# Block 1's v, q and g by three passes of split operands, in place of plain float32 matmuls

## The chip, the core and the metric

The kernel runs on one core of a Trainium2 chip. The metric is the device time of one execution in microseconds; before the change it is 929.19 us, the median of three runs (929.16 to 929.43).

## The reference

The input x is 4 sequences of 1024 tokens with 512 features, float32. Two sublayers follow each other, each with a layer norm before and after it and a residual sum:

```
h   = layernorm(x)
q, v, g = h @ Wq.T, h @ Wv.T, silu(h @ Wg.T)          # 512 x 512 each
ret = scan over tokens: state = lam * state + v       # lam per head of 32 features
out = (layernorm(q * ret) * gamma + beta) * g
x1  = x + layernorm(out @ Wo.T)

h2  = layernorm(x1)
f   = silu(h2 @ fp8(gate_w) * gate_s) * (h2 @ fp8(up_w) * up_s)   # 512 -> 1536
x2  = x1 + layernorm((f @ fp8(down_w)) * down_s)                  # 1536 -> 512
```

The FFN weights are rounded to an 8-bit float type and used as float32.

## The kernel before

The 4096 tokens are worked off in 8 blocks of 512 (TB). Each block goes through the first sublayer (class Retention) and then the FFN (class Ffn). The FFN of a block is a loop over 12 chunks of 128 hidden features (`for i in range(NI)`), in each of which TensorE does a gate group (pfg), an up group (pfu) and, two chunks later, a down group (pd), of 8 matmuls each. The work of the next block's first sublayer is placed by hand between the groups of this loop: `f` is the FFN of block t, `b` is the Retention of block t+1, `n` that of block t+2, and `l` is the FFN of the block before. All of it is in one program whose order is written out by hand: every engine takes its instructions in the order of the source (InOrder), so one instruction that waits holds up all that stand behind it on its engine, and SP issues all but a few DMAs in that order as well.

There are two ways to compute a product here. The plain one (project) multiplies float32 operands; blocks 0 and 1 use it for v, q, g and o (methods v, q, gate, o). The other one is by exact passes (begin, end, pass_of); blocks 2 to 7 use it. Each operand is cut into a top part (its upper mantissa bits), a low part (the rest) and a diff part (a combination of the two), of type F32R. `begin` does the top pass and the low pass into one bank of PSUM, after which ACT scales the bank by 1 + 4096; `end` adds the diff pass. A pass is four matmuls of 128x512. After `end`, v is scanned on DVE in two halves of 256, q is multiplied into y, and g goes through silu into the tile mids.

For the passes the weights must be split. Splitter does it in 16 units: n = 0 to 3 are the four 128-column chunks of v, 4 to 7 of q, 8 to 11 of g, 12 to 15 of o. `copy` copies a unit from its input to a DRAM tile (the top part), `split` computes low and diff by three DVE operations and one of ACT, `store` writes both to DRAM, and `keep` loads o's top and low. In the kernel before, the split overwrites the weights in SBUF (low takes the place of w), so a unit of v, q or g can be split only when block 1 has used it for the last time. The four units of o are split before the first FFN, and v, q, g during the FFN of block 0; two units of g are left for the FFN of block 1. From block 2 on, all parts are fetched from DRAM through a ring of four units (w_ring).

The FFN weights come in 18 pieces of 128x1024 (gate, up, down in turn; three pieces serve two chunks i). A piece is loaded into a scratch place (`parts[places[n]]`, seven places, of which four become the tile for x1nT of block 0 later), cast to the 8-bit type on DVE, and written as F32R into gate_sb, up_sb or down_sb by ACT. `rounds(k)` advances this by k steps, three to a piece. A piece whose place is taken is loaded when the piece before it in that place has been cast (load_next).

PSUM has eight banks: pa0 and pa1, two of pf, and pd0 to pd3. Gate and up of the FFN share the two pf banks: a gate group can start when ACT's silu has read the gate before it (or DVE the up before it), and so on in turn.

The order before the FFN of block 0 is: block 0's v and q; its g, interleaved with the transposition of block 1's x (turn_x, keep_x); block 1's v; block 0's o, one 128-token row set s after the other, with the moments of o (o_moments), the residual (x1_of), the moments of x1 (x1_moments), its normalised form (x1n_of) and its transposition (turn_x1n, upper_of, rest_of); and between these the first chunks of block 1's q. Pool does the variance roots and the residual sums. In the FFN of block 0 come the rest of block 1's q (i = 0, 1), the mean and g (i = 3 to 6), the normalisation of y (mean, center_y, var, rstd_y, z), and o (i = 7 to 10).

Of the kernel before, what the change touches and what calls it, by code (L numbers as in the profile page):

```python
# [23 lines left out]
def sandwich(  # L24
# [135 lines left out]
    places = [0, 4, 1, 5, 2, 6, 3] + [4 + n % 3 for n in range(len(pieces) - 7)]  # L160
# [169 lines left out]
    class Splitter:  # L330


        def __init__(self):
            self.sources = {"v": wvT, "q": wqT, "g": wgT, "o": woT}
            self.at_work = {}
# [7 lines left out]

        def copy(self, n):
            k, c = units[n]
            parts = operands[k, c] = {
                part: dram.tile([P, D], F32, tag=f"{part}_{k}{c}", name=f"d{part}_{k}{c}", bufs=1)
                for part in ("top", "low", "diff")
            }
            if k == "o":  # L350
                sp.dma_start(parts["top"], woT[ts(c, P), :])
            else:
                src = self.sources[k].rearrange("(c p) f -> p c f", p=P)[:, :, ts(c, P)]
                sp.dma_start(self.by_chunk(parts["top"]), src)

        def split(self, n):
            k, c = units[n]
            if k == "o":
                w, top, low = wo_sb[:, c], self.room[0], self.room[1]
            else:  # L360
                w = {"v": wv_sb, "q": wq_sb, "g": wg_sb}[k][:, :, ts(c, P)]
                top, low = self.by_chunk(self.room[n % 2]), w
            dve.tensor_scalar(top.bitcast(I32), w.bitcast(I32), TOP_MASK, None, ALU.bitwise_and)
            dve.tensor_tensor(low, w, top, ALU.subtract)
            dve.scalar_tensor_tensor(top, top, -LOW, low, ALU.mult, ALU.add)
            act.activation(low, low, AF.Copy, scale=1.0 / LOW)
            self.at_work[n] = top, low

        def store(self, n):
            k, c = units[n]  # L370
            for part, ap in zip(("diff", "low"), self.at_work.pop(n)):
                t = operands[k, c][part]
                sp.dma_start(t if k == "o" else self.by_chunk(t), ap)

        def keep(self, n):
            k, c = units[n]
            if c == 0:
                room = big.tile([P, 2, NC, D], F32R, tag="x1n0", name="wo_parts")
                wo_parts["top"], wo_parts["low"] = room[:, 0], room[:, 1]
            for part in ("top", "low"):  # L380
                sp.dma_start(wo_parts[part].bitcast(F32)[:, c], operands[k, c][part])

        times = {
            (0, 0, "start"): "k15 c0", (0, 0, "mid"): "s0", (0, 1, "start"): "k0", (0, 1, "mid"): "s1",
            (0, 1, "end"): "c1 c2", (0, 2, "start"): "k1 s2", (0, 2, "end"): "k2 c3",
            (0, 3, "end"): "s3 c4", (0, 4, "start"): "c5", (0, 4, "mid"): "k3 s4",
            (0, 4, "end"): "c6", (0, 5, "start"): "k4 s5", (0, 5, "mid"): "c7 k5", (0, 5, "end"): "s6 c8",
            (0, 6, "start"): "k6", (0, 6, "mid"): "s7 c9", (0, 6, "end"): "k7 s8",
            (0, 7, "start"): "s9", (0, 7, "mid"): "k8 k9", (0, 8, "end"): "c10", (0, 11, "end"): "c11",
            (1, 0, "start"): "r s10", (1, 0, "mid"): "s11 k10", (1, 0, "end"): "k11",  # L390
            (1, 2, "end"): "w12", (1, 3, "mid"): "w13", (1, 4, "mid"): "w14", (1, 5, "start"): "w15",
# [46 lines left out]
    class Retention:  # L438
# [7 lines left out]
        def __init__(self, t, xt=None):  # L446
# [6 lines left out]
            self.fast = t >= FAST  # L453
            self.bank, self.top, self.flipped = {}, {}, {}
# [16 lines left out]
        def new_xnT(self):  # L471
            kind = F32R if self.fast else F32
            self.xnT = big.tile([P, TB // Q, NC, Q], kind, tag="xnT", name=f"xnT_{self.t}")
# [25 lines left out]
        def keep_x(self, s, copy=act.copy):  # L499
            copy(self.by_chunk[:, :, ts(s, NQ)], self.ptx.pop(s).rearrange("p c (b j) -> p c b j", j=Q))  # L500

# [65 lines left out]
        def pass_of(self, bank, k, c, part):  # L567
            w = next_unit(k, c, part).rearrange("p (c f) -> p c f", c=NC)
# [8 lines left out]
            fetch_weights()  # L577
# [110 lines left out]
        def scan(self, c):  # L688
            home = big if self.t == 1 and c > 1 else work
            tag, bufs = ("fuse", 3) if home is big else ("ret", 2)  # L690
            self.ret[c] = ret = home.tile([P, TB], F32, tag=tag, name=f"ret_{self.t}_{c}", bufs=bufs)
# [83 lines left out]
        def silu(self, c):  # L775
            home = big if self.t == 0 and c == 3 else work
            tag, bufs = ("fuse", 3) if home is big else ("tok", 4) if self.t == 1 and c == 0 else ("sg", 3)
# [13 lines left out]
        def gate_y(self, c):  # L791
            y = self.y[:, c, :]
            if self.fast:
# [187 lines left out]
    for n in range(4):  # L981
        load_piece(n)
    wg_sb = load_square(wgT, "wg_sb")
# [5 lines left out]
    splitter = Splitter()  # L989
    splitter.new_room()  # L990
    a = Retention(0, x_first)
# [20 lines left out]
    b = Retention(1)  # L1012
    wo_sb = load_square(woT, "wo_sb")
    for n in range(4, 7):
        load_piece(n)
    a.v(0, "pf", later)
    a.scan(0)
    rounds(2)
# [4 lines left out]
    rounds(2)  # L1023
    a.q(1)
    a.y_of(1)
    rounds(2)
    a.v(2, "pf")
    a.scan(2)
    rounds(2)
    a.q(2)  # L1030
    a.y_of(2)
    rounds(2)
    a.v(3, "pf")
    a.scan(3)
    rounds(1)
    b.stats(0)
    a.q(3)
    a.y_of(3)
    for s in range(1, NS):
        b.stats(s)  # L1040
    splitter.copy(12)
    splitter.split(12)
    b.rstd()
    b.shift()
    a.g_of(0, "pf")
    a.mean()
    a.center_y()
    a.g_of(1, "pf")
    for s in range(NS):
        b.norm_x(s, True)  # L1050
    a.gate(2, "pf")
    b.new_xnT()
    for s in range(NS):
        b.turn_x(s, f"pd{s}")
    b.keep_x(0)
    b.keep_x(1)
    b.keep_x(2, dve.tensor_copy)
    b.keep_x(3, dve.tensor_copy)
    a.var()
    rounds(6)  # L1060
    a.rstd_y()
# [3 lines left out]
    splitter.store(12)  # L1065
    splitter.copy(13)
    b.v(0, "pf", early)
    b.v(0, "pf", later)
    for c in range(NC):
        a.z(c)  # L1070
    splitter.split(13)
    b.v(1, "pf")
    b.scan(0)
    b.v(2)
    b.scan(1)
    rounds(3)
    b.v(3, "pf")
    b.scan(2)
    rounds(1)
    b.scan(3)  # L1080
    splitter.store(13)
    splitter.copy(14)
    splitter.split(14)
    a.o(0, "pd0")
    a.o_moments(0)
    rounds(1)
    a.x1_of(0)
    a.o(1, "pd1")
    a.o_moments(1)
# [3 lines left out]
    a.o(2, "pd2")  # L1093
    a.o_moments(2)
    a.x1_moments(1)
    a.x1_of(2)
    a.x1n_of(1)
    a.o(3, "pd3")
    a.new_x1nT()
    a.turn_x1n(0)  # L1100
# [6 lines left out]
    b.q(0, "pf")  # L1107
    a.turn_x1n(1)
    a.upper_of(1)
    splitter.store(14)  # L1110
    splitter.copy(15)
    b.q(1, "pf", early)
    a.turn_x1n(2)
    a.upper_of(2)
    b.q(1, "pf", later)
    a.x1_moments(3)
    a.x1n_of(3)
    a.rest_of(1)
    b.y_of(0)
    a.rest_of(2)  # L1120
    rounds(2)
    a.turn_x1n(3)
    a.upper_of(3)
    b.q(2, "pd0", early)
    a.rest_of(3)
    rounds(1)
    b.y_of(1)
    splitter.split(15)

    l = None  # L1130
    for t in range(NB):
        f, n = Ffn(a), None
        fast = b is not None and b.fast
        for i in range(NI):
            if t > 0 and (t > 1 or i) and not (fast and i == 11):
                (f if i else l).rest((i - 1) % NI)
            if t == 0 and i == 0:
                n = Retention(2)
                rounds(3)
# [24 lines left out]
            if b and not fast and i == 5:  # L1164
                b.z(0)
            if b and not fast and i >= 8:
                b.x1_moments(i - 8)
            f.gate(i)
            if t == 0 and i in (5, 6):
                n.norm_x(2 * i - 10, True)  # L1170
                n.norm_x(2 * i - 9, True)
# [4 lines left out]
            if n and t == 0 and i == 7:  # L1176
# [20 lines left out]
            if b and t == 0 and i < 2:  # L1197
                b.q(i + 2, tokens=slice(None) if i else later)
                b.y_of(i + 2)
            if b and not fast and i == 3:  # L1200
                b.g_of(0)
                b.mean()
                b.center_y()
                n.stats(2)
# [3 lines left out]
            if b and not fast and i == 4:  # L1208
                rounds(3)
                b.g_of(1)  # L1210
                b.var()
            if b and not fast and i == 5:
                b.g_of(2)
                b.z(1)
            if b and not fast and i == 6:
                b.g_of(3)
                b.z(2)
                b.z(3)
            if b and not fast and 7 <= i <= 10:
                b.o(i - 7)  # L1220
            if b and not fast and i == 8:
                b.new_x1nT()
            if b and not fast and 8 <= i < 11:
                b.x1n_of(i - 8)
            if b and not fast and 8 <= i < 10:
                b.move_x1n(i - 8)()
            if b and not fast and 9 <= i < 11:
                b.upper_of(i - 9)
            if b and not fast and 7 <= i < 10:
                b.o_moments(i - 7)  # L1230
# [17 lines left out]
            if t == 0 and i == 10:  # L1248
# [3 lines left out]
            if b and i == 11:  # L1252
# [3 lines left out]
            if t == 0 and i == 11:  # L1256
# [8 lines left out]
            if t == 0 and i == 4:  # L1265
# [43 lines left out]
            if n and t == 0 and i in (8, 9):  # L1309
                n.low_of(2 * i - 16)  # L1310
                n.low_of(2 * i - 15)
            if n and t == 0 and i == 10:
# [9 lines left out]
            if t == 0:  # L1322
                if i == 3:
                    rounds(2)
                    b.halves()
                    rounds(1)
                elif i < 8:
                    rounds(3)
                if i == 2:
                    b.halves()  # L1330
# [10 lines left out]
            if n and i == 6:  # L1341
                n.new_xnT()
            if b and not fast and 7 <= i <= 10:
                b.x1_of(i - 7)
            if b and not fast and i >= 9:
                b.rest_of(i - 9)
# [5 lines left out]
            if t == 0 and i in (5, 6):  # L1352
# [181 lines left out]
```

## Time and profile before

| | |
|---|---|
| median of three runs | 929.19 us |
| the profiled execution, its own time | 930.15 us |
| span from its first to its last instruction | 928.3 us |
| mean granted TensorE clock | 0.990 |
| first gate group of block 0's FFN | 105.70 us from the span's start |
| first gate group of block 1's FFN | 217.96 us |
| TensorE waits from 0 to 105.7 us: for ACT's g | 8.5 us, once |
| TensorE waits from 105.7 to 218 us: pfg for ACT's gate | 5.7 us, 5 times |
| the same: pt for DVE's x1n | 4.6 us, once |
| TensorE waits from 218 us to the end | 1.4 us in all |

The profile is one execution, taken by the hardware profiler. Engines are PE (TensorE's matmuls), PEld (its weight loads), DVE (VectorE), ACT (ScalarE), POOL (GpSimd) and SP (SyncE, which issues DMAs). Line 75 is the helper through which all instructions go, so groups are told apart by tiles. A plain float32 matmul stands in the records as two, and a row of several matmuls overlaps the next row, since their ends are modelled: a group's price is read from one start to the next. What stands in brackets is the idle time before a row, and what ended it.

### The profile page before, as it was taken

Reading aid. Unit: us, or ns where it says so; the run is one execution under the profiler, and the core shown is the slowest. Engines: PE = TensorE matmul, PEld = TensorE weight load, DVE = VectorE, ACT = ScalarE, POOL = GpSimd, SP = SyncE. Lnnn points to the kernel's source line nnn. Section 1 sums busy time; section 2 is a strip of 40 time slices with the busy share of each in tenths; the row PEclk is TensorE's granted clock in tenths of the full one; section 3 lists DMA queues with packets and bytes.
Section 4 is the critical chain, followed back from the end, with each engine's and each line's share of the span. In section 5 each row is a group of like instructions: output and inputs, shape, how many; then the busy total and the mean of one; then the engine's idle time right before and its main releaser. Section 6 shows DMA issues by size and latency. Waiting matters only on the chain.

```text
span 928.3 us, 11878 instructions
## 1 busy us (share of the span) xinstructions
PE 895.1 (96%) x3924; PEld 737.0 (79%) x3924; DVE 618.0 (67%) x1057; ACT 416.6 (45%) x727; POOL 237.2 (26%) x304
## 2 busy tenths in 40 slices
PE   9969999998999999999999999999999999999995
PEld 7434666666888888888888888888888888888885
DVE  4545578677758766685758867687758765665545
ACT  2252556543364534544354434644355532644323
POOL 1212320130232304132141503332141502422020
PEclk9979999999999999999999999999999999999998
DMA  9512555647865467537656467456656274433021
GB/s 309 190 57 68 177 186 181 193 137 232 251 220 157 152 211 229 163 82 245 216 169 160 132 208 231 147 123 207 217 189 181 80 238 144 130 112 114 1 92 49
DMA packets 112474, 152.68 MB, mean 164 GB/s; under 512 B 10835, under 2 KB 50516, under 8 KB 112340
## 3 DMA queue, kind: packets, MB, share of 16 engines
q1 hardware_dynamic: 111540, 151.18, 53.2%
q10 hardware_dynamic: 864, 0.66, 0.2%
q8 instruction: 33, 0.54, 0.2%
q14 instruction: 37, 0.30, 0.1%
HBM read 116.41 MB, written 39.58 MB: 168 GB/s over the span
## 4 chain that ended last, share of the span: by engine, by line
PE 77%; DVE 10%; ACT 5%; DMA 4%; issue 2%; POOL 1%; SPq 0%; ACTq 0%; DVEq 0%
PE pfg L75 15%; PE pfu L75 15%; PE pd L75 14%; PE pv L75 10%; PE po L75 8%; PE pq L75 7%; PE pg L75 7%; DVE st L75 2%; DMA mx<-xs 2%; DVE split_room L75 1%; DVE y L75 1%; DVE gate L75 1%; ACT down_sb L75 1%; PE pt L75 1%; ACT L75 1%
## 5 line engine op out<-in xcount | busy, mean ns | idle before, releaser
L75 PE MATMUL pfg<-x1nT,gate_sb 128*128 128x512 f32 x768 | 183.0, 381 | 5.8 <-ACT gate L75 5.7
L75 PE MATMUL pfu<-x1nT,up_sb 128*128 128x512 f32 x768 | 184.1, 382 | 0.5 <-DVE gate L75 0.4
L75 PE MATMUL pd<-down_sb,fuse 128*128 128x512 f32 x720 | 170.5, 379 | 0.0
L75 PEld LDWEIGHTS pfg<-x1nT,gate_sb 128*128 128x128 f32 x768 | 144.2, 189 | 29.4 <-ACT gate L75 9.2
L75 PEld LDWEIGHTS pfu<-x1nT,up_sb 128*128 128x128 f32 x768 | 145.0, 189 | 24.8 <-issue 2.2
L75 PEld LDWEIGHTS pd<-down_sb,fuse 128*128 128x128 f32 x720 | 141.3, 196 | 14.6
L75 DVE SCALAR_TENSOR_TENSOR gate<-pfu,us_sb,gate 128x512 f32<-128x512 f32 x96 | 71.8, 748 | 66.2 <-PE pfu L75 54.6
L75 ACT CAST fuse<-gate 128x512 fp32r<-128x512 f32 x90 | 55.6, 618 | 130.0 <-DVE gate L75 129.7
L75 ACT ACTIVATE gate<-pfg,gs_sb 128x512 f32<-128x512 f32 x96 | 65.7, 684 | 95.2 <-PE pfg L75 95.2
L75 POOL TENSOR_SCALAR mv<-mv 128x1 f32<-128x1 f32 (+1 forms) x82 | 22.1, 270 | 336.3 <-DVE mv L75 334.3
L75 DVE TENSOR_TENSOR fuse<-gate,fuse 128x512 fp32r<-128x512 f32 x90 | 70.9, 787 | 5.8 <-ACT fuse L75 5.8
L75 POOL TENSOR_TENSOR d<-d,x 128x512 f32<-128x512 f32 x28 | 41.7, 1511 | 84.5 <-ACT d L75 70.6
L75 DVE BATCH_NORM_STATS2 st<-x 128x6 f32<-128x512 f32 x64 | 43.6, 681 | 18.0 <-POOL x L75 15.7
L75 POOL TENSOR_TENSOR mv<-mv,nhalf 128x1 f32<-128x1 f32 (+1 forms) x75 | 51.2, 683 | 6.3
L75 POOL TENSOR_TENSOR x<-x,x1n 128x512 f32<-128x512 f32 x32 | 45.3, 1423 | 19.5 <-ACT x1n L75 12.5
L75 PE MATMUL pv<-xnT,wv_sb 128*128 128x256 f32 (+1 forms) x88 | 31.2, 511 | 8.9 <-ACT g L75 8.5
L75 POOL TENSOR_TENSOR sqsum<-sqsum,sq 128x512 f32<-128x512 f32 x24 | 32.6, 1360 | 17.4 <-ACT sq L75 15.6
L75 POOL TENSOR_TENSOR ysum<-y 128x512 f32<-128x512 f32 x8 | 10.3, 1284 | 102.2 <-DVE y L75 102.2
L75 ACT ACTIVATE pv<-pv 128x512 f32<-128x512 f32 x24 | 14.0, 583 | 49.0 <-PE pv L75 49.0
L75 PEld LDWEIGHTS pv<-xnT,wv_sb 128*128 128x128 f32 x88 | 18.1, 209 | 21.1 <-ACT g L75 9.4
L75 DVE BATCH_NORM_STATS2 st<-po 128x6 f32<-128x512 f32 x32 | 22.0, 686 | 17.9 <-PE po L75 17.8
L75 POOL TENSOR_TENSOR ysum<-ysum,y 128x512 f32<-128x512 f32 x16 | 20.7, 1295 | 44.4 <-DVE y L75 44.4
(162 smaller groups left out, 1479.7 us busy)
## 6 DMA issues: line engine op xcount, KB each, us to landing
x<-in_x SPq DMA_DIRECT2D x52, 256.0 KB, 4.5
kept<-x SPq DMA_DIRECT2D x32, 256.0 KB, 2.0
x<-kept SPq DMA_DIRECT2D x32, 256.0 KB, 4.4
out<-d SPq DMA_DIRECT2D x31, 256.0 KB, 2.1
w_ring<-dtop_v SPq DMA_DIRECT2D x24, 256.0 KB, 3.1
w_ring<-dlow_v SPq DMA_DIRECT2D x24, 256.0 KB, 3.0
w_ring<-ddiff_v SPq DMA_DIRECT2D x24, 256.0 KB, 3.6
w_ring<-dtop_q SPq DMA_DIRECT2D x24, 256.0 KB, 2.7
```

The lines of the kernel that those rows point to most:

```text
L75: return lambda *args, **kwargs: tc.keep_in_program_order(op(*args, **kwargs))
```

## The change

Block 1's v, q and g are computed by passes, and g comes first. Block 1's x is cut into parts (cut_x, part_x). All three weights are loaded again in F32R form by way of their DRAM copies (load), and the splits leave them as they are: low and diff go to one of five slots, and the parts of x go to the second half of the FFN weights' tiles. Slots and parts stand where pieces 9 to 17 belong, which can be rounded only after block 1's last pass. The order is now: block 0's v, q, g; block 1's g; block 0's o; block 1's v and q between the row sets of o's tail; then the FFN. The 12 units of g, v, q are split before the FFN, those of o in the FFN of block 1. In the FFN of block 0, everything of block 1 and block 2 stands one chunk i earlier than before.

```diff
-    places = [0, 4, 1, 5, 2, 6, 3] + [4 + n % 3 for n in range(len(pieces) - 7)]
+    places = [n if n < 4 else 4 + (n - 4) % 3 for n in range(len(pieces))]
...
+        def new_slots(self):
+            pairs = [
+                big.tile([P, 2, TB], F32R, tag="fuse", name=f"slot_{n}", bufs=3) for n in range(2)
+            ]
+            pairs.append(down_sb[:, NI - 2 : NI, :])
+            self.slots = [(self.by_chunk(pair[:, 0]), self.by_chunk(pair[:, 1])) for pair in pairs]
+            for w in (gate_sb, up_sb):
+                self.slots.append((w[:, :, I - 2 * P : I - P], w[:, :, I - P : I]))
...
+        def load(self, k):
+            w = wpool.tile([P, NC, D], F32R, tag=f"w{k}_sb", name=f"w{k}_units")
+            for c in range(NC):
+                sp.dma_start(w.bitcast(F32)[:, :, ts(c, P)], self.by_chunk(operands[k, c]["top"]))
+            self.raw[k] = w
...
         def split(self, n):
...
-                w = {"v": wv_sb, "q": wq_sb, "g": wg_sb}[k][:, :, ts(c, P)]
-                top, low = self.by_chunk(self.room[n % 2]), w
+                w, top = self.raw[k].bitcast(F32)[:, :, ts(c, P)], self.by_chunk(self.room[n % 2])
+                low, diff = self.slot_of[k, c] = self.slots[len(self.slot_of) % len(self.slots)]
             dve.tensor_scalar(top.bitcast(I32), w.bitcast(I32), TOP_MASK, None, ALU.bitwise_and)
             dve.tensor_tensor(low, w, top, ALU.subtract)
-            dve.scalar_tensor_tensor(top, top, -LOW, low, ALU.mult, ALU.add)
-            act.activation(low, low, AF.Copy, scale=1.0 / LOW)
+            dve.scalar_tensor_tensor(diff, top, -LOW, low.bitcast(F32), ALU.mult, ALU.add)
+            act.activation(low, low.bitcast(F32), AF.Copy, scale=1.0 / LOW)
...
         times = {
...
+            (0, 1, "end"): "c12", (0, 2, "end"): "c13", (0, 3, "end"): "c14", (0, 4, "end"): "c15",
+            (1, 0, "mid"): "r w12 w13",
+            (1, 0, "end"): "w14 w15", (1, 1, "end"): "s12", (1, 2, "start"): "s13",
+            (1, 2, "end"): "k12 s14", (1, 3, "start"): "k13", (1, 3, "end"): "s15 k14",
+            (1, 4, "mid"): "k15",
...
+            if self.passes and not self.fast:
+                home = down_sb[:, NI // 2 : NI // 2 + NC, :]
+                self.xnT = home.rearrange("p a (g c j) -> p (a g) c j", c=NC, j=Q)
+                self.low, self.diff = (w[:, :, I // 2 : I // 2 + TB] for w in (gate_sb, up_sb))
...
+        def cut_x(self, s):
+            x = self.ptx.pop(s)
+            self.top[s] = top = work.tile([P, NC, P], F32, tag="tok", name=f"top_{self.t}_{s}", bufs=4)
+            dve.tensor_scalar(top.bitcast(I32), x.bitcast(I32), TOP_MASK, None, ALU.bitwise_and)
+            act.copy(self.by_chunk[:, :, ts(s, NQ)], top.rearrange("p c (b j) -> p c b j", j=Q))
+            dve.tensor_tensor(self.low[:, :, ts(s, P)], x, top, ALU.subtract)
+
+        def part_x(self, s):
+            low = self.low[:, :, ts(s, P)].bitcast(F32)
+            dve.scalar_tensor_tensor(
+                self.diff[:, :, ts(s, P)], low, -1.0 / LOW, self.top.pop(s), ALU.mult, ALU.add
+            )
...
+    for c, home in enumerate(("pa0", "pf", "pf", "pa1")):
+        b.begin("g", c, home)
     for c in range(NC):
         a.z(c)
+    for c in range(NC):
+        b.end("g", c)
+    splitter.split(1)
     rounds(3)
     a.o(0, "pd0")
+    splitter.split(2)
+    splitter.store(1)
+    rounds(3)
     a.o_moments(0)
...
+    b.begin("v", 0, "pf")
     a.turn_x1n(0)
...
+    b.begin("q", 3, "pf")
+    rounds(3)
+    b.end("q", 2)
+    rounds(3)
+    b.end("q", 3)
...
             if t == 0:
-                if i == 3:
-                    rounds(2)
+                if i == 0:
+                    rounds(3)
+                    b.halves()
+                    rounds(3)
+                elif i == 2:
+                    rounds(5)
                     b.halves()
                     rounds(1)
-                elif i < 8:
-                    rounds(3)
-                if i == 2:
-                    b.halves()
+                elif i < 6:
+                    rounds(6)
```

## The prediction

> **What bounds the kernel now.** I read the page's busy times first, then the clock by stage, then TensorE's timeline.
>
> ```profile
> PE 895.1 (96%) x3924; PEld 737.0 (79%) x3924; DVE 618.0 (67%) x1057; ACT 416.6 (45%) x727; POOL 237.2 (26%) x304
> ...
> PEclk9979999999999999999999999999999999999998
> ```
>
> TensorE is busy for 96%, so its 33 us of idle time and its work are all there is to win. The clock dips in one slice. By stages (columns: length; busy us of PE, PEld, DVE, ACT, POOL; clock; DMA share; GB/s):
>
> ```profile
> 37.60:65.10 27.50, 18.30 (x53) 8.13 (x52) 14.73 (x27) 15.54 (x23) 7.22 (x8) 0.90 0.14 48
> ...
> 105.70:218.00 112.30, 101.26 (x383) 72.90 (x382) 82.52 (x139) 57.27 (x98) 22.66 (x30) 0.98 0.59 178
> 218.00:325.20 107.20, 106.57 (x494) 92.64 (x493) 78.41 (x134) 50.97 (x89) 30.96 (x38) 1.00 0.66 208
> ```
>
> From 218 on (FFN of block 1 beside block 2) PE idles 0.6 us in 107: nothing to win there. Before 218 it idles some 22 us. The timeline shows where (start, length, [idle before]):
>
> ```profile
> 30.73 3.60 PE L75 MATMUL pv<-xnT,wv_sb 128*128 128x512 f32 x8
> 34.16 3.60 PE L75 MATMUL pq<-xnT,wq_sb 128*128 128x512 f32 x8
> 37.59 3.60 PE L75 MATMUL pg<-xnT,wg_sb 128*128 128x512 f32 x8
> ...
> 65.10 16.35 PE L75 MATMUL pv<-xnT,wv_sb 128*128 128x256 f32 x40 [8.53 <-ACT g L75]
> ```
>
> ```profile
> 205.03 1.03 PE L75 MATMUL pv<-xnT,w_ring 128*128 128x512 f32 x4
> 205.90 1.03 PE L75 MATMUL pv<-low,w_ring 128*128 128x512 f32 x4
> 206.76 1.89 PE L75 MATMUL pd<-down_sb,fuse 128*128 128x512 f32 x8
> 213.24 1.09 PE L75 MATMUL pt<-ident,x1n 128*128 128x128 f32 x4 [4.59 <-DVE x1n L75]
> 213.98 2.06 PE L75 MATMUL pv<-diff,w_ring 128*128 128x512 f32 x4
> ```
>
> Ends are modelled, so starts give the prices. One chunk of v, q or g by plain matmuls takes 3.43 us (34.16 to 37.59); one exact pass of four matmuls takes 0.865 (205.03, 205.90, 206.76), three 2.59. And the same diff pass took 1.85 us after the 4.59 us hole.
>
> ```profile
> 59.60:65.10 5.50, 0.00 (x0) 0.00 (x1) 4.66 (x9) 5.47 (x9) 0.00 (x0) 0.50 0.70 238
> 65.10:69.80 4.70, 4.70 (x11) 3.80 (x12) 3.87 (x6) 1.06 (x2) 0.00 (x0) 0.50 0.02 3
> ...
> 213.20:216.60 3.40, 3.36 (x10) 2.93 (x11) 1.91 (x3) 0.82 (x2) 0.00 (x0) 0.50 0.13 50
> ```
>
> Each long hole is followed by TensorE at half clock: 4.7 us, losing 2.35, and 3.4 us, losing 1.7.
>
> **Removed: arithmetic.** 12 units x (3.43 - 2.59) = 10.1 us, all on TensorE's path, in the same operand form that block 2 already runs.
>
> **Removed: the hole at 57.** Block 1's v needs the bank of g's third chunk, and its silu stands behind this on ACT:
>
> ```profile
> 58.60 1.28 ACT L75 ACT_TABLE_LOAD   x1 [0.92 <-DVE var L75]
> 59.90 0.32 ACT L75 ACTIVATE roots<-var,eps_sb 128x16 f32<-128x16 f32 x1
> 60.12 1.04 ACT L75 ACTIVATE up_sb<-scr 128x1024 fp32r<-128x1024 fp8e4 x1
> 61.07 0.18 ACT L75 ACTIVATION_READ_ACCUMULATOR up_sb<-scr 128x1 f32 x1
> 61.16 1.99 ACT L75 ACTIVATE down_sb<-scr 128x1024 fp32r<-128x1024 fp8e4 x1
> ```
>
> The new order puts both silus ahead of the root, and one rounding (1.04) ahead of them. I carried the four queues forward by hand with the rows' durations. Up to pg at 37.6 nothing moves on TensorE. Then g's split and its first rounding, its silu ends at 44.7, the four normalisations at 47.4, the squares and the second silu at 51.2; TensorE ends g at 54.6 and var at 55.5. DVE has cut all four x by 52.8 and split v0 by 54.6; ACT ends the two silus at 57.1 and 57.7. So g's begins run at 55.5, 57.2, 59.0, 60.7 and its ends at 62.4 to 65.9, with gaps of 0.2 at most. What is late next is z on DVE (8 x 0.72 from 60.3, to 66.2), and o's fourth matmul wants it only at 68.5. o of block 0 starts at 65.9; in the profile it starts at 81.3. Worth: 8.53 + 2.35.
>
> **Removed: the hole at 208.6.** Block 1's last moments start after o(3), which moves from i = 10 to 9. The chain from the end of o(3) to the transposed x1n is 10 to 11 us (moments 0.9, Pool 0.8, x1n 1.3, Pool's add 1.3, moments 0.9, Pool 0.8, x1n 0.6, and queueing); TensorE now has 15.6 us of work in between (three FFN groups of i = 9 and 10 and i = 11's), where it had 10.4. Worth 4.59 + 1.7. The small holes of that FFN, 6.3 us in all (5.7 of them pfg waiting for ACT's gate), are replaced below.
>
> **Added before the FFN.** Eight more units are split ahead of it than now. A split is on DVE 0.40 + 0.69 + 0.69 (1.8 us) and on ACT 0.63. From z's end at 66.2 to the last y, DVE has 7 splits (12.6), 7 casts (4.6), 8 moments (6.9), 4 rests (2.6), 8 half scans (6) and 4 products (2.6): 35.3 us of some 40. It is nearly full, and ACT's bank scalings (0.58), which every end waits for, queue behind x1n's chain and roundings. By hand I find four holes: 0.9 at v1's end (x1n of rows 2 is ahead of its scaling), 0.9 at q1's, 2.1 at q2's (the rounding of a down piece, 1.9), 0.1 at pfg: 4 us. The FFN then starts at about 106, as now (105.7), but with 5.5 units (18.9 us) less left in it.
>
> DMA: v, q, g are copied to DRAM and loaded again, some 6 MB more in the first 66 us. SP's queue is in program order; what might hold it is the copy before its load. g's load lands at about 22.5 (6 MB at the 308 GB/s of the first 37.6 us) and its split stands at 24.8; v's is issued at 34.2 behind a.v(3) and wanted at 53. Two us late would cost nothing: v2's scan, next on DVE, frees the bank that g(0) wants at 37.6. I price it 0 (0 to 3; a transfer more can't gain).
>
> **Added in the FFN of block 0.** g and q of block 1 were its padding: 18.9 us of TensorE work, beside which ACT rounded pieces. Now nine pieces (9 to 17, whose places held block 1's parts) and piece 8 must be rounded in i = 0 to 4. ACT per piece: 1.04, 1.04, 1.9. With gate (0.58) and fuse (0.52), halves, squares (4 x 0.57), two table loads (1.28) and two normalisations (1.5), ACT has 5, 6.7, 4, 7, 5.7 us in i = 0 to 4 where TensorE has 3.5, 3.9, 5.2, 5.6, 5.2: 28.4 against 23.4. The order adds to that: mu waits for a half that stands behind a down piece on ACT (111.4 to 113.3), var's likewise, with only pfg (1.73) in front of them instead of pfg and a g unit (5.2). By hand: 3.0 at mu, 0.4, 1.2, 1.8 at the pfgs and pfus around it, 2.8 at var, 0.8 at i = 5 and 6. I take 10 us; the bounds are 5 (5.0 of ACT's surplus alone) and 14 (every piece landing late: 512 KB land in 6 to 7 us and three places rotate).
>
> **The clock's rule.** In the trace a hole of 1.70 us left the clock alone, 4.59 and 8.53 halved it. The Trainium skill, "TensorE: Matmul & The Clock Gate", section "Why this matters for your kernels", says to leave no idle gap over about 3 us, since one idle window (3.4 us, by Part 1 of that page) halves the clock. My holes at mu and var are 2.8 to 3.0, between the two. By the rows, free; by the rule's strict side, each costs half of 3.4, together 3.4. They are nearer to 1.70, so I take 0, and keep 3.4 for the range.
>
> **Moved into block 1's FFN.** The four o splits replace two g splits: 2 x 1.8 on DVE and 1.3 on ACT more, where DVE idles 5.7 us between 229 and 253 and the splits come to 7.2. I take 1.5 (0 to 4).
>
> **Sum**, against the profiled execution (span 928.3; its own time 930.15, 1.0 over the median 929.19): -10.1 - 10.9 - 6.3 - 6.3 = -33.6; +4 + 10 + 1.5 = +15.5; net -18.1. The walk by stages gives block 1's FFN a start at 106 + 38.6 (i = 0 to 5: 28.6 of work and 10 of holes) + 34.5 (four iterations of 5.2 with an o of 3.43) + 0.7 (a wait there) + 5.2 + 10.0 (i = 11 with five passes and pt) = 195.0 instead of 217.96; with the 1.5 that is -21.5. The midpoint is near -19.5: span 908.8, median 909.7, rounded to 910.
>
> **Rivals.**
> 1. *The squeeze doesn't reach TensorE.* ACT's lag is caught by two spare banks: 5 instead of 10 in the FFN, 2 instead of 4 before it, nothing in block 1: 910 - 8.5 = 901.5. For it: ACT is only 45% busy. Against: pfg shares two banks with pfu, and five of the eight holes in that FFN now are exactly that wait. 0.13.
> 2. *The squeeze costs more*: both holes lengthen until the clock falls (3.4), and half of the delay of rival 3 comes on top (8): 921. 0.18.
> 3. *Slower: DVE's queue is the bound from 66 on.* 20 of its instructions there wait for another engine. In 85 to 105 now, nine such waits cost 9.6 us, 1.07 each. If they stay and splits don't fill them, DVE ends at 66.2 + 35.3 + 20 x 1.07 = 123, 16 later than in my walk (107), and the change gains 3.5. It turns slower from 1.25 us a wait on; at 1.4 it is 932. Against: these waits now are DVE having nothing else to do. 0.06.
> 4. *No difference*: 0.03, on the way from 2 to 3. That the passes don't run at 0.865 is excluded by the same form at 205.
>
> **Chances.** The likeliest, 0.60: 905 to 916, time 910. With 1 and 2 the range is 901 to 922. A measurement here tells 0.2% (1.9 us) from no change. Faster 0.91, same 0.03, slower 0.06.
>
> **What would show it.** Twelve units in passes of 0.865 from 55 to 105; no PE hole over 3 us before 106 and clock 1.00 there; o of block 0 at about 66; first pfg at 104 to 108; 8 to 12 us of PE idle between that and i = 6, most before mu, var and pfg, released by ACT or DVE half; no hole before pt at i = 11; block 1's FFN starting at about 197. Wrong if g's first split waits for its DMA beyond 28, if DVE ends the last q product after 112, or if the clock falls in the FFN.

## The result and the profile after

The changed kernel takes 924.64 us (median; 923.53 to 926.11), the kernel before 929.37 us on the same chip: a ratio of 0.9947, 95% interval 0.9934 to 0.9960. It is faster, by 4.7 us and not by the 19.5 of the forecast; 910 was predicted, and the range of 901 to 922 doesn't hold the time. The profiled execution has a span of 922.8 us (its own time 924.62).

First the page's busy times and clock of the changed kernel:

```profile
PE 888.1 (96%) x3948; PEld 742.6 (80%) x3948; DVE 629.1 (68%) x1071; ACT 424.7 (46%) x741; POOL 239.8 (26%) x304
...
PEclk9999999999899999999999999999999999999999
```

TensorE's work has shrunk by 7 us, its share has not grown. The dip of the clock at slice 3 has gone, and one at slice 11 (231 to 254 us) is new. So I cut both traces at the first gate group of each block's FFN (times in us; the experiments' rows are used further down):

| profiled execution of | before block 0's FFN | block 0's FFN | block 1's FFN | the rest | span |
|---|---|---|---|---|---|
| before | 105.7 | 112.3 | 107.1 | 603.2 | 928.3 |
| prediction's walk | 106 | 89.0 | 108.6 | 603.2 | 906.8 |
| after | 108.8 | 91.1 | **118.7** | 604.2 | 922.8 |
| o's splits left out | 109.2 | 92.0 | 106.4 | 604.6 | 912.1 |
| second split later | 108.6 | 91.0 | 115.1 | 603.6 | 918.3 |
| first store earlier | 109.2 | 90.9 | 118.3 | 603.4 | 921.8 |
| both | 108.7 | 91.1 | 112.8 | 604.1 | 916.6 |
| both, fourth split later | 108.7 | 90.7 | 107.9 | 603.3 | 910.6 |
| splits spread | 108.9 | 92.2 | 109.4 | 602.6 | 913.1 |

At the start of block 1's FFN the change is 18.1 us ahead of before (199.91 against 217.96). At its end 6.4 are left. This is a stage in which the kernel before idled for 0.6 us. Here is TensorE's timeline of the changed kernel in it:

```profile
232.70 2.07 PE L75 MATMUL pq<-diff,w_ring 128*128 128x512 f32 x4 [4.14 <-ACT pq L75]
...
248.07 0.49 PE L75 MATMUL mu<-half,mean_r 128*128 128x512 f32 x1 [3.31 <-ACT half L75]
...
259.58 0.49 PE L75 MATMUL var<-half,mean_r 128*128 128x512 f32 x1 [0.83 <-ACT half L75]
```

Three holes, 8.3 us, and two of them halve the clock behind them (the columns are those of the prediction's tables by stages):

```profile
232.20:235.60 3.40, 2.90 (x7) 2.36 (x8) 0.85 (x3) 0.45 (x1) 0.00 (x0) 0.50 0.02 5
249.30:252.70 3.40, 3.40 (x9) 2.70 (x9) 3.37 (x5) 1.97 (x4) 3.29 (x3) 0.50 0.35 134
```

That is 1.7 us lost in each, 3.4 in all. The stage is 11.6 us longer than before: in it TensorE idles 8.7 us against 0.6, and is busy for 110.0 us against 106.5, which is the half clock. So the holes and their clock are the whole of the loss. What they wait for stands on ACT and DVE. First ACT, ahead of the hole at 232.70:

```profile
230.06 0.63 ACT L75 ACTIVATE wo_parts<-wo_parts 128x512 fp32r<-128x512 f32 x1 [6.52 <-DVE split_room L75]
231.54 0.62 ACT L75 CAST fuse<-gate 128x512 fp32r<-128x512 f32 x1 [0.85 <-DVE gate L75]
232.07 0.58 ACT L75 ACTIVATE pq<-pq 128x512 f32<-128x512 f32 x1
```

`wo_parts` is the ACT step of o's second split (s13). ACT stands still for 6.52 us before it, with the cast to fuse and the scaling of q's bank queued behind; this bank was complete at 226.7, and TensorE's diff pass wants the scaling. DVE shows why s13 is late:

```profile
224.23 2.47 DVE L75 TENSOR_TENSOR d<-pd,ds_sb 128x512 f32<-128x512 f32 x4
...
227.22 0.41 DVE L75 TENSOR_SCALAR split_room<-wo_parts 128x512 int32<-128x512 int32 x1
227.66 1.64 DVE L75 TENSOR_TENSOR wo_parts<-wo_parts,split_room 128x512 fp32r<-128x512 f32 x1
...
240.93 0.43 DVE L75 TENSOR_SCALAR split_room<-wo_parts 128x512 int32<-128x512 int32 x1 [4.54 <-DMA ddiff_o<-split_room]
```

The transpositions of block 3's x and the four down scalings of block 0 (d) are ahead of it: DVE doesn't idle, the wanted work stands too far behind. One step of s13 also takes 1.64 us here, against 0.69 in run 2, since Pool adds beside it (see the last section). The last line is the third split, s14. It waits 4.54 us for the store of the first one's diff, since both use the same one of two rooms. SP issued that store late:

```profile
234.80 0.32 SPq L75 DMA_DIRECT2D w_ring<-dtop_g  x1
...
237.39 0.42 SPq L75 DMA_DIRECT2D ddiff_o<-split_room  x1
```

It is queued behind fetches for the ring, which wait until the stalled TensorE has freed a unit. So the store delays a split, the split the moments of d behind it on DVE, these Pool's roots and the last sum of y behind them, and this sum `half`, for which mu waits 3.31 us:

```profile
244.31 0.20 POOL L75 TENSOR_SCALAR mvd<-mvd 128x4 f32<-128x4 f32 x1 [7.32 <-DVE mvd L75]
...
246.11 1.26 POOL L75 TENSOR_TENSOR ysum<-ysum,y 128x512 f32<-128x512 f32 x1
...
247.40 0.62 ACT L75 CAST half<-ysum 128x512 fp32r<-128x512 f32 x1 [0.79 <-POOL ysum L75]
```

Whether the store is late only because of the first hole, as I took it at first, run 2 tells.

### The profile page after: what moved, and what is told of

Same layout as the page of the kernel before. It is cut to its first block, busy times and chain, and to the rows that moved or that the text cites. A ratio compares the mean times of both kernels' runs of the same rounds, so it can differ in the third digit from the quotient of the medians.

```text
span 922.8 us, 11982 instructions
## 1 busy us (share of the span) xinstructions
PE 888.1 (96%) x3948; PEld 742.6 (80%) x3948; DVE 629.1 (68%) x1071; ACT 424.7 (46%) x741; POOL 239.8 (26%) x304
## 5 line engine op out<-in xcount | busy, mean ns | idle before, releaser
L75 ACT ACTIVATE pv<-pv 128x512 f32<-128x512 f32 x28 | 16.3, 582 | 54.1 <-PE pv L75 54.1
L75 POOL TENSOR_TENSOR ysum<-y 128x512 f32<-128x512 f32 x8 | 10.8, 1347 | 108.6 <-DVE y L75 108.6
L75 DVE TENSOR_TENSOR y<-pq,y 128x512 f32<-128x512 f32 x28 | 19.1, 681 | 23.0 <-PE pq L75 23.0
L75 DVE SCALAR_TENSOR_TENSOR y<-y,lnb_sb,mids 128x512 f32<-128x512 f32 x28 | 27.0, 965 | 7.1 <-ACT mids L75 7.0
L75 ACT ACT_TABLE_LOAD x19 | 24.4, 1283 | 16.0 <-DVE var L75 11.5
```

The lines of the kernel that those rows point to most:

```text
L75: return lambda *args, **kwargs: tc.keep_in_program_order(op(*args, **kwargs))
```

## Experiments

Three theories: A, the loss is one of order, made by the places at which o's splits and stores stand in three queues; B, it is one of amount, since DVE and ACT have no room for four splits in this stage, wherever they stand; C, it comes from something other than the splits. Each run is beside the kernel before on its own chip (930.97 to 931.77 us in these runs, 929.37 beside the change); gains are read from the ratios, and that of the change is 0.9947.

**1. o's splits left out.** No unit of o is split or stored; its low and diff are loaded from the top part instead, so o of blocks 2 to 7 is another product of the same size.

```diff
+            sp.dma_start(wo_parts["low"].bitcast(F32)[:, c], operands[k, c]["top"])
+            operands[k, c]["diff"] = operands[k, c]["top"]
...
-            (1, 0, "mid"): "r w12 w13",
-            (1, 0, "end"): "w14 w15", (1, 1, "end"): "s12", (1, 2, "start"): "s13",
-            (1, 2, "end"): "k12 s14", (1, 3, "start"): "k13", (1, 3, "end"): "s15 k14",
-            (1, 4, "mid"): "k15",
+            (1, 0, "mid"): "w12 w13",
+            (1, 0, "end"): "w14 w15",
```

> The changed kernel without the work of o's four splits in block 1's FFN: DVE and ACT leave them out, o's low and diff parts are loaded from the unsplit weights (so o of blocks 2 to 7 is computed from parts that aren't split), and the four stores become four loads. Theory A (the 12.5 us lost behind 199.9 us come from these splits): block 1's FFN takes 107 us again instead of 118.7, no hole over 1 us and no half clock in it, time 913 (911 to 915). Rival B (the splits only add DVE load where DVE was nearly full): the same, 913. Rival C (the loss comes from elsewhere in that FFN, such as the weights' ring or the phase of its loads): at least 922.

Measured: 912.99 us, ratio 0.9802 (0.9786 to 0.9819). Block 1's FFN takes 106.4 us. TensorE's waits from its start to the end of the span are now (us in total, times, longest):

```profile
PE pq L75 <- ACT pq L75: 1.3, 3, 0.5
PE pfg L75 <- ACT gate L75: 0.2, 1, 0.2
```

C falls: all the time that is missing is with o's splits and their stores, 12.3 us of this stage.

**2. The second split a moment later**, behind the down scalings.

```diff
-            (1, 0, "end"): "w14 w15", (1, 1, "end"): "s12", (1, 2, "start"): "s13",
+            (1, 0, "end"): "w14 w15", (1, 1, "end"): "s12", (1, 2, "mid"): "s13",
```

> Only the second o split is moved, from the start of i = 2 to behind that chunk's begin of q, so that its ACT scaling stands behind q2's bank scaling. Same DVE work. Theory A (order in ACT's and SP's queues): the 4.14 us hole before q2's diff pass and its half clock go, and with TensorE not held up the store that the third split waits for is issued earlier, so that most of the hole at mu goes too: 916 (914 to 919). Rival B (7.2 us of DVE work where DVE had 5.7 idle: throughput): the work is the same, so at most 2 us better: 922.5 or more. Rival C: 924.

Measured: 920.58 us, ratio 0.9889 (0.9871 to 0.9907), some 5.4 us under the change. It lies between the theories: A said 916 (914 to 919), B 922.5 or more. The hole before q falls from 4.14 to 0.94 us, but the store stays late and mu waits 3.80:

```profile
229.64 1.13 PE L75 MATMUL pq<-diff,w_ring 128*128 128x512 f32 x4 [0.94 <-ACT pq L75]
244.07 0.49 PE L75 MATMUL mu<-half,mean_r 128*128 128x512 f32 x1 [3.80 <-ACT half L75]
```

```profile
233.37 0.42 SPq L75 DMA_DIRECT2D ddiff_o<-split_room  x1
```

```profile
236.91 0.43 DVE L75 TENSOR_SCALAR split_room<-wo_parts 128x512 int32<-128x512 int32 x1 [4.46 <-DMA ddiff_o<-split_room]
```

So the second hole stands without the first, though I had read it as its consequence: even with TensorE on time, SP comes to this store at 233.37, behind the ring's fetches, and s14 waits 4.46 us for it.

**3. The first store earlier**, ahead of the second split and of the ring's fetches; the split stays.

```diff
-            (1, 0, "end"): "w14 w15", (1, 1, "end"): "s12", (1, 2, "start"): "s13",
-            (1, 2, "end"): "k12 s14", (1, 3, "start"): "k13", (1, 3, "end"): "s15 k14",
+            (1, 0, "end"): "w14 w15", (1, 1, "end"): "s12", (1, 2, "start"): "k12 s13",
+            (1, 2, "end"): "s14", (1, 3, "start"): "k13", (1, 3, "end"): "s15 k14",
```

> Only the store of the first o split's diff part is moved forward, from the end of i = 2 to its start, ahead of the ring's fetches that wait for TensorE. Theory A: the 4.14 us hole stays, DVE no longer waits 4.5 us for that store before the third split, and the hole at mu (3.3) with its half clock goes or shrinks under 1: 920 (918 to 922). Rival B: unchanged within 1 us, 924. Rival C: 924.

Measured: 922.97 us, ratio 0.9907 (0.989 to 0.9923): 3.7 us under the change by the ratio. A had said 920 (918 to 922), which is 4.6 under the change's 924.64, B and C 924, as good as no gain. By itself this is not decisive, since 922.97 lies between them; the trace tells more. mu's hole is gone, q's is as it was, and another has grown:

```profile
232.89 2.07 PE L75 MATMUL pq<-diff,w_ring 128*128 128x512 f32 x4 [4.15 <-ACT pq L75]
...
257.64 0.49 PE L75 MATMUL var<-half,mean_r 128*128 128x512 f32 x1 [2.54 <-ACT half L75]
```

In the change mu came so late that the fourth split (s15), which stands between mu and var, was half hidden. With mu on time it is in the way of var: 2.54 us and 1.7 of half clock. Besides, the half clock behind q's hole lasts 6.83 us here (from 232.27) instead of 3.41, another 1.7. So in this profiled execution the stage is only 0.4 us shorter than in the change.

**4. The splits spread out**: loads and the first split earlier, one split at each of four places, each store close behind its split, the fourth split behind var.

```diff
-            (1, 0, "mid"): "r w12 w13",
-            (1, 0, "end"): "w14 w15", (1, 1, "end"): "s12", (1, 2, "start"): "s13",
-            (1, 2, "end"): "k12 s14", (1, 3, "start"): "k13", (1, 3, "end"): "s15 k14",
-            (1, 4, "mid"): "k15",
+            (0, 11, "mid"): "r w12 w13 w14 w15",
+            (1, 0, "start"): "s12", (1, 0, "mid"): "k12 s13", (1, 0, "end"): "k13 s14",
+            (1, 1, "start"): "k14", (1, 5, "start"): "s15", (1, 5, "mid"): "k15",
```

> All four o splits stay, but stand where DVE was idle: o's top parts are loaded at the end of block 0's FFN, three splits are in i = 0 of block 1's FFN and one at the start of i = 5, each store right behind the next split. Theory A: all three half-clock windows go, block 1's FFN takes 107 to 109 us, time 913 to 915. Rival B (throughput): i = 0 to 2 together still carry 5.4 us more DVE work than before the change, so a hole of 2 to 4 us comes back there: 917 to 920. Rival C: 924.

Measured: 914.81 us, ratio 0.9821 (0.9804 to 0.9837). The stage takes 109.4 us, a little over A's 107 to 109, without half clock. The same four splits cost 3.1 us in it instead of 12.3. B falls.

**5. Both edits of 2 and 3 together**: the store k12 at the start of i = 2, the split s13 at its middle.

> The change with both edits of the two experiments before: the second o split behind the down scalings, and the store of the first one ahead of it. Theory A (each wait was a loss of its own): the two gains add up, 5.4 + 3.7 us, 917, ratio 0.985 (0.984 to 0.987), with the fourth split still between mu and var. Theory C (one chain, so that one edit took most of the other's gain): 0.988 or more. If the fourth split counts for nothing: 0.982.

Measured: 918.79 us, ratio 0.9868 (0.9848 to 0.9889). That is 7.4 us under the change, where the two gains add up to 9.1. The interval alone holds A's 0.985 and the 0.988 at which the one chain of the expectation's theory C would begin; the trace decides. Both holes are nearly gone (1.4 us before q, 0.2 before mu), and the largest that is left is the one before var:

```profile
PE var L75 <- ACT half L75: 2.5, 1, 2.5
```

**6. Besides, the fourth split behind var** (the edit is against the change).

```diff
-            (1, 0, "end"): "w14 w15", (1, 1, "end"): "s12", (1, 2, "start"): "s13",
-            (1, 2, "end"): "k12 s14", (1, 3, "start"): "k13", (1, 3, "end"): "s15 k14",
-            (1, 4, "mid"): "k15",
+            (1, 0, "end"): "w14 w15", (1, 1, "end"): "s12", (1, 2, "start"): "k12",
+            (1, 2, "mid"): "s13", (1, 2, "end"): "s14", (1, 3, "start"): "k13", (1, 3, "end"): "k14",
+            (1, 5, "start"): "s15", (1, 5, "mid"): "k15",
```

> The change with the two edits together, and besides the fourth o split taken out from between mu and var to the start of i = 5 (its store a moment later). Theory A: this split is the third loss: the hole of 2.54 us before var and the 1.7 us of half clock behind it go, 4.2 us, so the ratio falls from 0.987 to 0.982 or 0.983, as with the spread splits. If var still waits, or another wait takes its place: 0.985 or more.

Measured: 913.05 us, ratio 0.9814 (0.9798 to 0.983). var waits no more. With three splits or stores moved by a few places the stage takes 107.9 us, 1.5 over the kernel without splits, and the kernel is some 12 us faster than the change.

**7. The kernel before with its silus first**: only this reordering, no passes.

```diff
-    a.var()
-    rounds(6)
-    a.rstd_y()
     a.silu(2)
     a.gate(3, "pf")
     a.silu(3)
+    a.var()
+    rounds(6)
+    a.rstd_y()
```

> The kernel before, with block 0's two last silus of g and its last g product moved ahead of the variance's root and of the roundings; no passes, nothing else. Theory A (the step of the prediction): the 8.53 us hole before block 1's v and the 2.35 us lost to half clock behind it were a matter of ACT's order alone, so both go and the ratio to before is 0.988 (0.986 to 0.990). Theory B: v keeps waiting, now for a later instruction of ACT or DVE, and less than half is gained: 0.994 or more. Under A the passes and the rest of the change earn only what is left.

Measured: 925.85 us, ratio 0.9938 (0.9919 to 0.9958): outside A's range and at the edge of B's, but not for B's reason. The hole of 8.53 us and the half clock behind it are gone, v starts at 57.70, and the FFN of block 0 starts 8.0 us sooner. Of these 3.1 are given back by its i = 2, where 4.9 are left. This kernel's second gate group and what ACT does ahead of it:

```profile
106.42 3.78 PE L75 MATMUL pfg<-x1nT,gate_sb 128*128 128x512 f32 x8 [3.17 <-ACT gate L75]
```

```profile
102.37 1.99 ACT L75 ACTIVATE down_sb<-scr 128x1024 fp32r<-128x1024 fp8e4 x1
...
104.39 1.28 ACT L75 ACT_TABLE_LOAD   x1
105.68 0.69 ACT L75 ACTIVATE gate<-pfg,gs_sb 128x512 f32<-128x512 f32 x1
```

In the kernel before a silu followed the root, so silu's table was loaded in the shadow of the hole of 8.53 us:

```profile
63.16 1.28 ACT L75 ACT_TABLE_LOAD   x1
```

With the silus first the load of 1.28 us falls behind the first gate group: the wait there grows from 1.70 to 3.17, and the clock is halved for 6.8 us behind it (105.4 to 112.2). Even so, moving three lines gains as much by itself as the whole change does (0.9938 against 0.9947).

**8 and 9. Block 0's FFN.** The spread splits of 4, with `b.halves()` ahead of the roundings at i = 0 and 2 (8); besides, the down piece's rounding behind the bank scalings of q2 and q3 (9).

```diff
-                    rounds(3)
                     b.halves()
-                    rounds(3)
+                    rounds(6)
...
-                    rounds(5)
                     b.halves()
-                    rounds(1)
+                    rounds(6)
```

and for 9

```diff
-    rounds(3)
     b.begin("q", 2, "pf")
     b.end("q", 1)
     b.begin("q", 3, "pf")
     rounds(3)
     b.end("q", 2)
-    rounds(3)
+    rounds(6)
     b.end("q", 3)
```

> As the kernel with spread splits and early halves and scalings, but the roundings before the FFN stand where the change has them; so it tells the halves from the scalings. Theory A: the holes at mu and var shrink by 4 us and their half clock (3.4) goes: ratio 0.974 to 0.976, with q2's hole and its half clock still there. Theory B (ACT short of time): 0.979 to 0.982.

> The change with its o splits spread over the free places of block 1's FFN, both halves (of mu and of var) of block 1 ahead of the roundings in block 0's FFN, and the roundings behind the bank scalings of q2 and q3 ahead of it. Theory A: these three holes (1.9, 2.3, 3.5 us) and the three stretches of half clock behind them (1.7 each) were a matter of ACT's order: some 10 us below the spread splits alone, about 904, ratio 0.970 to 0.974. Theory B: ACT and DVE are short of time in that stage, and what is moved behind is waited for by the gate groups instead: 0.979 to 0.982, as with the spread splits alone.

Measured: 913.00 us, ratio 0.9804 (0.9784 to 0.9824), for 8, and 912.54 us, ratio 0.9796 (0.9776 to 0.9816), for 9; against 4's 0.9821 neither is told apart for sure. That is B's time. Here are TensorE's waits from 105 to 152 us, first with the spread splits alone, then in 9:

```profile
PE var L75 <- ACT half L75: 3.5, 1, 3.5
PE mu L75 <- ACT half L75: 2.3, 1, 2.3
PE pq L75 <- ACT pq L75: 1.9, 1, 1.9
```

```profile
PE pfg L75 <- ACT gate L75: 6.2, 3, 2.6
PE var L75 <- ACT half L75: 1.3, 1, 1.3
PE pfu L75 <- DVE y L75: 0.9, 1, 0.9
```

Besides, the pfgs waited 1.9 us with the spread splits. mu waits 0.4 in 9, and q2 not at all: the three waits that were aimed at shrink by 6 us, and 5 come back before pfg and pfu, where ACT has the roundings now. The second gate group's silu in 9, for instance, stands behind two of them, of which the first waits for a cast of DVE, and TensorE's third gate group waits for it:

```profile
114.71 2.04 ACT L75 ACTIVATE down_sb<-scr 128x1024 fp32r<-128x1024 fp8e4 x1 [1.36 <-DVE scr L75]
...
117.66 0.67 ACT L75 ACTIVATE gate<-pfg,gs_sb 128x512 f32<-128x512 f32 x1
```

```profile
118.38 1.99 PE L75 MATMUL pfg<-x1nT,gate_sb 128*128 128x512 f32 x8 [2.03 <-ACT gate L75]
```

B's reason, that ACT and DVE are short of time, is not shown by this. From the first gate group to that of i = 5 (106.43 to 141.41) ACT is busy for 25.8 of 35.0 us in 9, DVE for 26.4 and TensorE for 25.7, and ACT stands idle for 4.3 us until casts of DVE come and for 4.0 until its gate products do. What the two runs show is that these two orders only move the waits; whether a third would end them stays open.

## Why the prediction failed

**The step that failed** is "Moved into block 1's FFN": "DVE idles 5.7 us between 229 and 253 and the splits come to 7.2. I take 1.5 (0 to 4)". It measured 11.6 us against before and 12.3 against the kernel without splits. Adding it to the stages in the table: the walk's 906.8, 2.8 for a later start, 2.1 for block 0's FFN, 10.1 for this stage beyond the walk's 108.6, and 1.0 for the rest give 922.8, the measured span. Without the 10.1 the time would have been inside the range.

A price of this size can be reached, as run 6 shows (107.9, against 106.4 without splits and 107.1 before). That it meets the 1.5 is in part luck: the 1.5 is work less DVE's idle time (5.7; the trace's busy times give 5.5), no run shows that this difference sets the cost, and at the places of run 4 the same work costs 3.1. What was wrong is that I compared an amount of work with an amount of idle time. Ahead of block 0's FFN the eight splits were carried through four queues by hand; for these four that was left out. It should have shown ACT's step of s13 with q's bank scaling behind it, and s14 sharing a room with a store that stands behind the ring's fetches.

**Point by point.**

- The passes run at 0.86 to 0.87 where nothing waits (starts at 62.08, 62.94, 63.81), as priced. g's first split starts at 25.24 right behind DVE's own work, not behind its DMA, so the DMA's price of 0 held.
- The hole at 57 went, as carried forward: o of block 0 starts at 68.12 (66 forecast, 81.3 before; the row stands below), and the clock is 1.00 up to 133 us. Run 7 shows the reordering alone to be worth 8.0 us at that point. The 2.2 that are missing: block 0's first g product is 0.6 late (38.16), a wait of 1.11 for a normalised x follows, the rest is in small gaps.
- The hole at 208.6 went: pt at i = 11 starts at 196.88 without a wait.
- Ahead of the FFN: 0.91 (v1), 0.41 (q0), 1.92 (q2), where 0.9, 0.9 (q1) and 2.1 were foretold. The first gate group is at 108.83, just outside the foretold 104 to 108.
- In block 0's FFN TensorE idles 8.8 us before i = 6 (10 foretold), before mu 2.26 + 0.23 (3.0), var 3.48 + 0.23 (2.8), the pfgs and pfus 2.6. The rows bear out the order foretold, mu's half behind a down piece on ACT. That ACT's amount of work is the ground, 28.4 us against 23.4, is not shown: up to the gate group of i = 5 ACT is busy for 24.4 of 36.0 us and TensorE for 27.0 (1.7 of it half clock), with the last two of the ten pieces still to come; see also runs 8 and 9.
- The clock: I took 0 for mu and var, and kept 3.4. mu cost nothing, var 1.7 (half clock from 133.2 to 136.6). Of the prediction's signs of being wrong this one came true, "if the clock falls in the FFN", here and twice in block 1's.
- Rival 1 is out, since the squeeze did reach TensorE. Rival 2 gave 921, close to the result, but for another place: block 0's FFN cost only 2.1 more than forecast. Rival 3, DVE as the bound from 66 on, is out: DVE ended the last q product at 110.0 where the walk had 107, not 16 us late, and the FFN started 2.8 late.

```profile
68.12 13.90 PE L75 MATMUL po<-wo_sb,y 128*128 128x512 f32 x32
...
116.55 0.49 PE L75 MATMUL mu<-half,mean_r 128*128 128x512 f32 x1 [2.26 <-ACT half L75]
...
132.84 0.50 PE L75 MATMUL var<-half,mean_r 128*128 128x512 f32 x1 [3.48 <-ACT half L75]
```

```profile
114.06 1.96 ACT L75 ACTIVATE down_sb<-scr 128x1024 fp32r<-128x1024 fp8e4 x1
...
115.89 0.60 ACT L75 CAST half<-ysum 128x512 fp32r<-128x512 f32 x1
```

## What to carry to other kernels

Work that is moved into a stage with spare time is to be priced by the queues, not by the sum: for each of its instructions, on each engine, write down what is just ahead of it (it waits for that) and who needs what is just behind it. Splits that cost 1.5 us at good places cost 12 at bad ones, a few instructions away. If a buffer is shared by two of the moved steps, the place of the store between them counts like an instruction of its own, and a fix that uncovers the next wait (s13, then the store, then s15) is worth judging only when all three are made.

## What was not expected of the hardware

**The clock.** How long a hole is doesn't decide alone; where it lies does. The starts of all stretches at half clock within one trace lie at whole multiples of 3.413 us from each other (in the kernel before 59.62 and 213.21: 45 of them; in the changed one 133.24 and 232.23: 29). The Trainium skill, "TensorE: Matmul & The Clock Gate", section "What's actually happening", tells of such a free-running window of 3413 ns, and the traces agree. I laid this grid over the eleven profiles and summed the bracketed idle time within each window. At full clock, a window with 1.91 us or more of it was always followed by one at half clock (1.91, 1.91, 1.92, 2.03, 2.16, 2.26 are the smallest), and one with 1.89 or less was not (1.89, 1.84, 1.81, 1.77, 1.70 are the largest), but for one of run 3 (1.71), which I can't explain. Back to full it went after a half-clock window with 0.47 us or less of idle time, and not with 0.62 (run 3, 232.27) or 1.01 (run 7, 105.42). So the hole of 2.26 before mu was free in the changed kernel, where an edge at 116.17 cut it, and cost 1.7 us in run 1, where it lay within one window, as did the 1.91 before q2. The rule that the prediction weighed, no gap over about 3 us, is too lax for this kernel: where a hole of 2 to 3 us lies in the grid decided over 1.7 us. It tilts the comparisons too: ahead of block 1's FFN the changed kernel and run 6 were at half clock for one window, runs 1 and 4 for three. Two windows lose 3.4 us of TensorE's clock, and that stage starts 1.1 to 1.7 us later in runs 1 and 4 (201.17 and 201.05, against 199.91 and 199.45), which goes with run 6 having a shorter span than run 1, which has no splits at all.

**DVE beside Pool.** The three DVE steps of the fourth split in the changed kernel, Pool's work beside them, and the same three steps in run 4:

```profile
251.73 1.24 DVE L75 TENSOR_SCALAR split_room<-wo_parts 128x512 int32<-128x512 int32 x1
253.00 1.65 DVE L75 TENSOR_TENSOR wo_parts<-wo_parts,split_room 128x512 fp32r<-128x512 f32 x1
254.69 1.64 DVE L75 SCALAR_TENSOR_TENSOR split_room<-split_room,wo_parts 128x512 f32<-128x512 f32 x1
```

```profile
251.42 4.36 POOL L75 TENSOR_TENSOR sqsum<-sqsum,sq 128x512 f32<-128x512 f32 x3
```

```profile
256.63 0.42 DVE L75 TENSOR_SCALAR split_room<-wo_parts 128x512 int32<-128x512 int32 x1
257.08 0.69 DVE L75 TENSOR_TENSOR wo_parts<-wo_parts,split_room 128x512 fp32r<-128x512 f32 x1
257.81 0.69 DVE L75 SCALAR_TENSOR_TENSOR split_room<-split_room,wo_parts 128x512 f32<-128x512 f32 x1
```

The three take 4.5 us while Pool adds squares, and 1.8 in run 4, where Pool is idle from 250.7 to 261.5. Each of the slow steps ends 0.3 to 0.6 us after one of Pool's three additions (252.97, 254.66 and 256.33 behind 252.69, 254.10 and 255.78). Just before, at 249.33, four DVE products with an operand in PSUM kept their 0.62 each beside Pool's additions. The Trainium skill, "SBUF — State Buffer", section "SBUF: two separate sides", tells of a port that Vector and GpSimd share and lock for a whole instruction; these rows fit it. A DVE price taken from a row without Pool's work beside it can be out by a factor of 2.4 to 3.0.
